# Attention scores of a sequence issued in two runs on TensorE instead of three

## The chip, the cores and the metric

The kernel runs on one core of one Trainium2 chip. A core has five engines that run side by side: TensorE (PE, matrix products), VectorE (DVE), ScalarE (ACT, functions of one variable), GpSimd (POOL) and SyncE (SP, which issues most of the DMA transfers). The metric is the device time of one execution in microseconds; the median of three executions of the kernel before is 3600.9 us (3593.78 to 3604.1).

## The reference

The input `x` is 32 sequences of 256 tokens with 256 channels. A state-space block works on it first, and then two transformer layers with local attention; the result is added to `x`.

```python
def _L0_cond_ref(x, t_emb, ...):
    xr, gate = jnp.split(x @ W_in.T, 2, axis=-1)
    ...                       # + t_emb, causal convolution of 4 taps, silu, layer norm -> xn
    def step(h, inputs):      # one step per token: 256 steps in a row
        ad, bd, xt, ct = inputs
        h = jnp.clip(h * ad[:, :, None] + bd[:, :, None] * xt[:, None, :], -10.0, 10.0)
        yt = jnp.einsum('bd,bdh->bh', ct, h)
        return (h, yt)
    ...
    return y * jax.nn.silu(gate) @ W_out.T

def _layer(x, wqkv, qs, ksc, wo, lg, lb, w1, b1, w2, b2):     # twice (DEPTH = 2)
    h = shift_token(x)
    q, k, v = jnp.split(h @ wqkv, 3, axis=-1)                 # 8 heads of 64
    q, k = l2norm(q) * qs, l2norm(k) * ksc
    q, k = rotary_xpos(q, k)
    o = local_attention(q, k, v)      # windows of 128: a query sees keys at most 128 back
    x = x + o @ wo
    h = layer_norm(shift_token(x))
    a, g = jnp.split(h @ w1 + b1, 2, axis=-1)                 # 682 wide each
    return x + (a * gelu(g)) @ w2 + b2

x = x + _L0_ffn_ref(_L0_cond_ref(x, cond, ...), ...)
```

With 256 tokens a sequence has two windows of 128. Keys of block 0 are seen by the queries of both windows, with a triangular mask in each half; keys of block 1 are seen by the queries of window 1 alone, with one triangular mask.

## The kernel before

**Tiling.** The 32 sequences form four groups of eight. The state-space block of a group is a scan of 256 steps. Each step is one VectorE instruction (`step`, L716) on a tile of 128 x 512; it needs a row of inputs that a DMA repeats over the partitions (`load_rows`, L685, tile `xrep`) and ScalarE scales (`scale_row`, L706). Four steps at a time, TensorE reads the states out into the tile `y` (`read_out`, L728). Around the scan stand its convolution (L478, L489, `th` at L504, `xc` at L509), a norm, a gate and two projections.

The two transformer layers of a group take its sequences one by one. Over the four groups that makes 64 sequence passes. They run one group behind the scan: while the sequences of group g are in attention and feed-forward, the scan of group g+1 goes on between them. The last group (`self.apart`) has no scan beside it.

**Stages.** A sequence pass takes eight stages (`ST = 8`). `stage(n, i, what)` puts a step of sequence n into stage i; a stage number of n+1, n+2 or n+3 means that the step of sequence n runs while a later one is in its attention. The stages that matter here are these:

- `turn` (stages 6 and 0): TensorE turns the queries and keys of a window; ScalarE copies them to `qT` and `kT` (L1033).
- `project` (stages 0 and 1 for window 0, 3 and 4 for window 1, of the next sequence): TensorE makes `ps_qkv` (L989), ScalarE squares it (L1002), VectorE and GpSimd rotate and normalise it (L1005 to L1022).
- `scores` (L1182): see below.
- `mask` (L1219): GpSimd clears the masked half of the second block's exponentials (L1225). In the last group VectorE does the same for the first block (L1230).
- `sums` and `values` (stage 7): TensorE sums the exponentials (`rs`, L1239) and multiplies them with the values (`ov`, L1258).
- `finish` (stage 6 of the next sequence): TensorE multiplies with `wo` (`ps_wo`, L1039).
- `normalise`, `apply`, `spread` (stages 0, 1 and 3, two sequences later): `tp_h`, `hn`, `tp_hn`, `hT`.
- `widen` for m = 0 to 5 (stages 4 to 9, two sequences later): TensorE makes `pa` (L1362), ScalarE takes the Gelu of one half (`ag`, L1373). One stage after each, `product` (L1380) on VectorE multiplies the other half into `ag`, and so ends the use of the PSUM bank of `pa`.
- `narrow` (stages 3 and 4, three sequences later): TensorE makes `po_f` (L1389), VectorE adds it to the residual (L1400).

**Scores.** A call `scores(b, kw, i0, n)` takes key block `kw` and n pairs of heads from pair i0 on. It opens two PSUM banks, one for each head of a pair, since a head has 64 channels and TensorE takes two heads side by side in the two halves of its rows. For block 0, outside the last group, a bf16 matmul first writes the mask into each bank (L1194); the products of keys and queries (L1205) then add to it in pieces of 64 keys and 192 queries. Block 1, and block 0 in the last group, have no mask in the bank and use pieces of 128 keys. Then ScalarE takes the exponentials of both banks (L1214) into tiles `pT`. A sequence has three calls: block 1 with all four pairs at stage 2, block 0 with pairs 0 and 1 at stage 3, and block 0 with pairs 2 and 3 at stage 5.

**Function tables.** [...] The exponential and the Gelu stand in different sets; where one follows the other, the built program has an instruction that loads a table (`ACT_TABLE_LOAD`).

**What sets the order.** After each stage the main loop (L1521) lets the scan advance by its share of steps, so the program's text interleaves both. The framework's scheduler then orders each engine's instructions, mostly in that order, and an engine runs its own list in order. All PSUM tiles come from one pool of eight banks (`ps_w`), used in turn: a tile's first writer waits until the last reader of the tile that had its bank is done. The six `pT` buffers hold one sequence's exponentials.

Of the kernel before, what the change touches and what calls it, by code (L numbers as in the profile page):

```python
# [10 lines left out]
FP = mybir.dt.float32  # L11
# [8 lines left out]
P = 128  # L20
S = 256
# [15 lines left out]
HEADS = 8  # L37
DH = 64
W = 128
# [13 lines left out]
def bc(ap, axis, n):  # L53

    ap = ap.unsqueeze(axis)
    shape = list(ap.shape)
    shape[axis] = n
    return ap.broadcast_to(shape)
# [15 lines left out]
def kernel(  # L74
# [29 lines left out]
    nc = tc.nc  # L104
# [72 lines left out]
    mask_t = const.tile([P, 2 * W], BF, tag="mask_t", name="mask_t")  # L177
    ident_b = const.tile([P, P], BF, tag="ident_b", name="ident_b")
# [43 lines left out]
    def program(ctx, exact):  # L222
# [9 lines left out]
        ps_w = ctx.enter_context(tc.tile_pool(name="psw", bufs=8, space=PSUM, reuse_waits="tile"))  # L232
# [921 lines left out]
        class Attention:  # L1154
# [24 lines left out]
                        self.rot.pop((b, w, a)), self.qkv[b][a][:, :, w * W : (w + 1) * W]  # L1179
                    )  # L1180

            def scores(self, b, kw, i0, n):  # L1182


                qT, kT, _ = self.qkv[b]
                nq = S - kw * W
                masked = kw == 0 and not self.apart
                nm = 2 if masked else 1
                mk = W // nm
                banks = []  # L1190
                for r in range(2):
                    sc = ps_w.tile([P, n, nq], FP, tag="w", name="sc")
                    if masked:
                        nc.tensor.matmul(  # L1194
                            sc, ident_b, bc(mask_t[:, 0:nq], 1, n), start=True, stop=False
                        )
                    banks.append(sc)
                for i in range(n):
                    for r in range(2):
                        rows = slice(r * DH, (r + 1) * DH)  # L1200
                        for m in range(nm):

                            k0 = m * mk
                            q0, q1 = (k0, k0 + W + mk) if masked else (0, nq)
                            nc.tensor.matmul(  # L1205
                                banks[r][k0 : k0 + mk, i, q0:q1],
                                kT[rows, i0 + i, kw * W + k0 : kw * W + k0 + mk],
                                qT[rows, i0 + i, kw * W + q0 : kw * W + q1],
                                start=not masked,
                                stop=not masked or i == n - 1,  # L1210
                            )
                for r in range(2):
                    p = aw.tile([P, n, nq], FP, tag="pT", name="pT", bufs=6)
                    nc.scalar.activation(p, banks[r], AF.Exp)  # L1214
                    self.ps[kw, i0, r] = p
                    for i in range(n):
                        self.p[b, kw, i0 + i, r] = p[:, i, :]
# [224 lines left out]
        def stage(n, i, what, *args):  # L1442
            stages.setdefault(ST * n + i, []).append(partial(what, *args))

        def attend(n, at, b, nxt):

            stage(n, 0, at.turn, b, 1)
            stage(n, 3, at.scores, b, 0, 0, 2)
            stage(n, 2, at.scores, b, 1, 0, HEADS // 2)
            stage(n, 5, at.scores, b, 0, 2, 2)  # L1450
            stage(n, 3, at.mask, 1, 0)
            if at.apart:
                for i, what in ((4, (0, 0)), (6, (0, 2))):
                    stage(n, i, at.mask, *what)
            stage(n, 7, at.sums, b)
            stage(n, 7, at.values, b)
            stage(n + 1, 0, at.put_inverse)
            stage(n + 1, 2, at.load_inverse)
            stage(n + 1, 4, at.divide, b)
            stage(n + 1, 6, at.finish, b)  # L1460
            if nxt is not None:
                for w in range(NW):
                    for i, a in ((0, 2), (1, 0), (1, 1)):
                        stage(n, 3 * w + i, nxt[0].project, nxt[1], w, a)
                stage(n, 6, nxt[0].turn, nxt[1], 0)
# [27 lines left out]
        for n, (g, l, b) in enumerate(seqs):  # L1493
            nxt = (ats[n + 1], seqs[n + 1][2]) if n + 1 < len(seqs) else None
            attend(n, ats[n], b, nxt)
            feed(n, g, l, b)
# [24 lines left out]
        for t in range(max(stages) + 1):  # L1521
# [3 lines left out]
            g, r = divmod(t + 1 + group - reload, group)  # L1525
# [124 lines left out]
```

## Time and profile before

| What | Value |
| --- | --- |
| Median of three executions | 3600.9 us |
| Profiled execution | 3604.19 us |
| Its span, from first to last instruction | 3602.5 us |
| TensorE busy | 3463.1 us |
| VectorE busy | 2667.7 us |
| ScalarE busy | 2148.9 us |
| GpSimd busy | 1884.7 us |
| TensorE clock granted, mean | 0.989 |

A profile row of a group of instructions gives line, engine, operation, output and inputs, shapes and count; then the busy time of the group, the mean duration of one in ns, and the time for which the engine stood idle just before them, with what ended it. In a list of waits the waiting instruction stands before the arrow, what it waited for behind it, and then the total in us, the number of times and the longest. The chain of waits starts at the last instruction and goes back, at each step to what released it or to the instruction before it on its engine. TensorE takes a float32 matmul in two passes, so the profile counts two for each.

The first 500 us belong to the scan of group 0, before any attention. From about 510 us on the 64 sequence passes follow each other; about 2630 us in, the scan of the last group is over.

### The profile page before, as it was taken

Reading aid. Unit: us, or ns where it says so; the run is one execution under the profiler, and the core shown is the slowest. Engines: PE = TensorE matmul, PEld = TensorE weight load, DVE = VectorE, ACT = ScalarE, POOL = GpSimd, SP = SyncE. Lnnn points to the kernel's source line nnn. Section 1 sums busy time; section 2 is a strip of 40 time slices with the busy share of each in tenths; the row PEclk is TensorE's granted clock in tenths of the full one; section 3 lists DMA queues with packets and bytes.
Section 4 is the critical chain, followed back from the end, with each engine's and each line's share of the span. In section 5 each row is a group of like instructions: output and inputs, shape, how many; then the busy total and the mean of one; then the engine's idle time right before and its main releaser. Section 6 shows DMA issues by size and latency. Waiting matters only on the chain.

```text
span 3602.5 us, 57609 instructions
## 1 busy us (share of the span) xinstructions
PE 3463.1 (96%) x20220; PEld 2254.4 (63%) x20220; DVE 2667.7 (74%) x5049; ACT 2148.9 (60%) x3659; POOL 1884.7 (52%) x1842
## 2 busy tenths in 40 slices
PE   7999988999999999999999999999999999999999
PEld 4545335666666666666666666666666677777777
DVE  5888889878888777887787888877877545555553
ACT  4656656666666666666666666666666544444543
POOL 4433466545556555655565556555544444443451
PEclk9999999999999999999999999999999999999999
DMA  7788755444454545444454555544454212011111
GB/s 201 210 217 219 200 154 148 133 110 138 131 140 130 149 140 146 130 114 126 117 140 128 135 149 137 142 106 130 116 141 123 61 38 61 13 30 39 31 27 37
DMA packets 468766, 435.67 MB, mean 121 GB/s; under 512 B 228723, under 2 KB 308084, under 8 KB 468340
## 3 DMA queue, kind: packets, MB, share of 16 engines
q1 hardware_dynamic: 384018, 419.88, 42.4%
q10 hardware_dynamic: 84450, 12.01, 2.0%
q8 instruction: 163, 2.67, 0.3%
q14 instruction: 135, 1.11, 0.1%
HBM read 383.54 MB, written 46.66 MB: 119 GB/s over the span
## 4 chain that ended last, share of the span: by engine, by line
PE 59%; DVE 19%; POOL 7%; DMA 7%; ACT 5%; issue 3%; SPq 0%; ACTq 0%; DVEq 0%; POOLq 0%
PE ps_qkv L989 12%; PE pa L1362 12%; DVE h L716 7%; PE po_f L1389 7%; DMA xrep<-xnd 5%; PE ps_wo L1039 4%; PE y L728 4%; PE ov L1258 3%; PE sc L1205 3%; DVE acc L489 3%; PE ps_out L808 2%; ACT xrep L706 2%; PE tr_qk L1028 2%; PE ps_in L399 2%; POOL rn L1021 2%
## 5 line engine op out<-in xcount | busy, mean ns | idle before, releaser
L716 DVE CUSTOM_DVE_ANT_0 h<-h,xrep,lim 128x512 f32<-128x512 f32 x1024 | 959.2, 937 | 219.2 <-ACT xrep L706 185.1
L706 ACT ACTIVATE xrep<-xrep,beta 128x512 f32<-128x512 f32 x960 | 674.2, 719 | 366.6 <-DMA xrep<-xnd 281.3
L989 PE MATMUL ps_qkv<-qkv,res 128*128 128x512 f32 x1536 | 718.5, 603 | 25.2 <-DVE ag L1380 9.8
L1362 PE MATMUL pa<-hT,w 128*128 128x256 f32 (+1 forms) x2816 | 679.9, 383 | 0.0
L1362 PEld LDWEIGHTS pa<-hT,w 128*128 128x128 f32 (+1 forms) x2816 | 516.2, 189 | 147.0 <-issue 53.8
L1013 POOL TENSOR_TENSOR rot<-rot,swp 128x512 f32<-128x512 f32 x256 | 340.1, 1328 | 442.7 <-DVE swp L1010 297.8
L989 PEld LDWEIGHTS ps_qkv<-qkv,res 128*128 128x128 f32 x1536 | 281.2, 191 | 314.1 <-issue 239.4
L1021 POOL TENSOR_TENSOR rn<-ss,neg_half 128x8 f32<-128x8 f32 x256 | 459.0, 1793 | 17.0 <-DVE ss L1019 6.9
L728 PE MATMUL y<-h,ly 128*32 128x512 f32 x2048 | 347.0, 611 | 18.9 <-DVE h L716 17.5
L1314 POOL TENSOR_TENSOR rstd<-ve,neg_half 128x2 f32<-128x2 f32 x64 | 47.0, 734 | 605.1 <-DVE ve L1312 587.7
L1389 PE MATMUL po_f<-ag,w 128*128 128x256 f32 x1280 | 309.7, 389 | 5.5 <-DVE fo L1400 4.3
L1022 POOL TENSOR_TENSOR rot<-rot,rn 128x512 f32<-128x512 f32 x256 | 289.3, 1130 | 19.9
L1380 DVE SCALAR_TENSOR_TENSOR ag<-pa,b_sb,ag 128x256 f32<-128x256 f32 x320 | 152.2, 476 | 195.8 <-ACT ag L1373 195.8
L1389 PEld LDWEIGHTS po_f<-ag,w 128*128 128x128 f32 x1280 | 237.3, 192 | 70.8 <-DVE xc L509 11.7
L1002 ACT ACTIVATE sq<-ps_qkv 128x512 f32<-128x512 f32 x256 | 151.9, 595 | 208.1 <-PE ps_qkv L989 145.5
L1373 ACT ACTIVATE ag<-pa,b_sb 128x256 f32<-128x256 f32 x320 | 150.1, 469 | 179.5 <-PE pa L1362 177.4
L489 DVE SCALAR_TENSOR_TENSOR acc<-xr,wc_sb,acc 128x256 f32<-128x256 f32 x384 | 197.7, 543 | 68.2 <-POOL acc L478 67.6
L1039 PE MATMUL ps_wo<-oT,wo 128*128 128x256 f32 x1024 | 231.6, 379 | 0.0
L1005 DVE TENSOR_TENSOR rot<-ps_qkv,rc_sb 128x512 f32<-128x512 f32 x256 | 174.5, 681 | 68.1 <-ACT sq L1002 67.9
L1214 ACT ACTIVATE pT<-sc 128x512 f32<-128x512 f32 x384 | 208.4, 596 | 6.8 <-PE sc L1205 4.8
L1039 PEld LDWEIGHTS ps_wo<-oT,wo 128*128 128x128 f32 x1024 | 194.6, 190 | 27.1 <-PE y L728 0.8
L1205 PEld LDWEIGHTS sc<-qT,kT 64*64 64x64 f32 (+1 forms) x2816 | 134.8, 159 | 114.6 <-issue 89.2
(159 smaller groups left out, 5689.8 us busy)
## 6 DMA issues: line engine op xcount, KB each, us to landing
xrep<-xnd SPq DMA_DIRECT2D x960, 256.0 KB
rb<-inv SPq DMA_DIRECT2D x128, 256.0 KB
xnd<-xn SPq DMA_DIRECT2D x64, 256.0 KB
qkv<-in_wqkv_dram SPq DMA_DIRECT2D x24, 512.0 KB
ahead<-xs_a SPq DMA_DIRECT2D x48, 256.0 KB
xp<-ahead SPq DMA_DIRECT2D x48, 256.0 KB
xd<-xnd SPq DMA_DIRECT2D x192, 64.0 KB
w<-in_w_dram SPq DMA_DIRECT2D x80, 128.0 KB
```

What stands on the lines that cost most here:

```text
L489: nc.vector.scalar_tensor_tensor(acc, xr[:, :, k : k + CH], wc_sb[:, ch, k : k + 1], acc, ALU.mult, ALU.add,)
L706: scaled = nc.scalar.activation(bx, ck[c].pop(("bx", t), bx), AF.Copy, scale=ck[c]["beta"][:, t : t + 1])
L716: nc.vector._custom_dve(TENSOR_ADD_SAT, out=h_new, in0=state["h"], in1=bx, s0=ck[c]["lim"][:, 0, t : t + 1], s1=ck[c]["lim"][:, 1, t : t + 1],
L728: nc.tensor.matmul(ck[c]["y", hb][32 * q : 32 * q + 32, :], ly[hb % 2][:, 32 * t : 32 * t + 32], ck[c].pop(("h", hb * TB + t)), start=(i = ...
L989: nc.tensor.matmul(ps, res[b][:, k, t0 : t0 + W], wt["qkv", a][:, k], start=(k == 0), stop=(k == KM - 1),)
L1013: nc.gpsimd.tensor_add(rot, rot, swp)
L1021: nc.gpsimd.tensor_tensor(rn, ss, neg_half, ALU.pow)
L1022: nc.gpsimd.tensor_mul(rot, rot, bc(rn, 2, DH))
L1039: nc.tensor.matmul(po[:, d], wt["wo", 0][:, c, d * P : (d + 1) * P], oT[:, c, :], start=(c == 0), stop=(c == NC_ - 1),)
L1205: nc.tensor.matmul(banks[r][k0 : k0 + mk, i, q0:q1], kT[rows, i0 + i, kw * W + k0 : kw * W + k0 + mk], qT[rows, i0 + i, kw * W + q0 : kw * ...
L1362: nc.tensor.matmul(dst[x], wt["w1", m][:, k, x], self.h[:, k], start=(k == 0), stop=(k == KM - 1),)
L1389: nc.tensor.matmul(self.po[:, d], wt["w2", 0][:, m, d * P : (d + 1) * P], self.ag[m], start=(m == 0), stop=(m == len(MCH) - 1),)
```

## The change

`scores` takes several parts at once. It opens the banks of all its parts and writes their masks (`open_banks`), then issues the products of all (`products`), and then the exponentials of all (`exponentials`). The bodies of the three are those of the old `scores`. At stage 2 the first half of block 0 goes together with block 1, block 0 first; the second half of block 0 goes from stage 5 to stage 3. In the last group the masks of block 0 move from stages 4 and 6 to stages 3 and 4. A sequence so has two runs of scores, of four banks and of two, where it had three of two banks.

```diff
-            def scores(self, b, kw, i0, n):
+            def open_banks(self, kw, n):
+                nq = S - kw * W
+                banks = []
+                for r in range(2):
+                    sc = ps_w.tile([P, n, nq], FP, tag="w", name="sc")
+                    if kw == 0 and not self.apart:
+                        nc.tensor.matmul(
+                            sc, ident_b, bc(mask_t[:, 0:nq], 1, n), start=True, stop=False
+                        )
+                    banks.append(sc)
+                return banks
+
+            def scores(self, b, *parts):
+                opened = [self.open_banks(kw, n) for kw, i0, n in parts]
+                for part, banks in zip(parts, opened):
+                    self.products(b, *part, banks)
+                for part, banks in zip(parts, opened):
+                    self.exponentials(b, *part, banks)
+
+            def products(self, b, kw, i0, n, banks):
                 qT, kT, _ = self.qkv[b]
                 nq = S - kw * W
                 masked = kw == 0 and not self.apart
                 nm = 2 if masked else 1
                 mk = W // nm
-                banks = []
-                for r in range(2):
-                    sc = ps_w.tile([P, n, nq], FP, tag="w", name="sc")
-                    if masked:
-                        nc.tensor.matmul(
-                            sc, ident_b, bc(mask_t[:, 0:nq], 1, n), start=True, stop=False
-                        )
-                    banks.append(sc)
                 for i in range(n):
...
+
+            def exponentials(self, b, kw, i0, n, banks):
+                nq = S - kw * W
                 for r in range(2):
                     p = aw.tile([P, n, nq], FP, tag="pT", name="pT", bufs=6)
                     nc.scalar.activation(p, banks[r], AF.Exp)
...
             stage(n, 0, at.turn, b, 1)
-            stage(n, 3, at.scores, b, 0, 0, 2)
-            stage(n, 2, at.scores, b, 1, 0, HEADS // 2)
-            stage(n, 5, at.scores, b, 0, 2, 2)
+            stage(n, 2, at.scores, b, (0, 0, 2), (1, 0, HEADS // 2))
+            stage(n, 3, at.scores, b, (0, 2, 2))
             stage(n, 3, at.mask, 1, 0)
             if at.apart:
-                for i, what in ((4, (0, 0)), (6, (0, 2))):
+                for i, what in ((3, (0, 0)), (4, (0, 2))):
                     stage(n, i, at.mask, *what)
```

## The prediction

> **What bounds the kernel now.** I read in turn the busy table and its 40 slices, the busy time by stretches, the waits of TensorE, ScalarE's groups, and the chain with the timelines of one pair of sequences (times of day below are from these timelines).
>
> The busy table:
>
> ```profile
> PE 3463.1 (96%) x20220; PEld 2254.4 (63%) x20220; DVE 2667.7 (74%) x5049; ACT 2148.9 (60%) x3659; POOL 1884.7 (52%) x1842
> ...
> PE   7999988999999999999999999999999999999999
> ```
>
> TensorE is the bound; only what it waits for, or streams, can move the end. By stretches, its idle time is 54 us before 500 us (attention has not begun: outside the change), 36 us from 500 to 1260, 41 us from 1260 to 2630, and 7 us afterwards. The stretch of 41 us, and what TensorE waited for in it:
>
> ```profile
> 1260.00:2630.00 1370.00, 1328.87 (x8267) 877.83 (x8260) 1097.29 (x2085) 886.34 (x1517) 793.19 (x736) 1.00 0.48 131
> ...
> PE sc L1194 <- DVE ag L1380: 18.7, 12, 2.2
> PE ps_qkv L989 <- DVE ag L1380: 9.8, 13, 0.9
> PE ov L1258 <- DVE ag L1380: 6.2, 10, 1.0
> PE ps_qkv L989 <- DVE rinv L1247: 3.1, 7, 0.5
> ```
>
> Nearly half is the mask matmul of a sequence's third score run (stage 5), which waits for a PSUM bank that `product` (L1380) frees late. It recurs every 103 us, in one of every two sequences.
>
> ScalarE's groups:
>
> ```profile
> L1214 ACT ACTIVATE pT<-sc 128x512 f32<-128x512 f32 x384 | 208.4, 596 | 6.8 <-PE sc L1205 4.8
> L1214 ACT ACT_TABLE_LOAD x124 | 159.1, 1283 | 7.1 <-PE sc L1205 4.4 <-ACT xrep L706 0.7
> L1373 ACT ACT_TABLE_LOAD x124 | 159.1, 1283 | 2.2
> ```
>
> The exponentials and the Gelu take turns: 124 loads each way for 64 sequences, about two of each per sequence, because the third run at stage 5 stands between `widen` at stages 4 and 6.
>
> The chain of waits from 1540 to 1602 us runs on TensorE to 1545.2, leaves it for VectorE, GpSimd and ScalarE, and returns at 1595.75. Some of it:
>
> ```profile
> 1578.12 0.61 ACT xrep L706
> ...
> 1578.75 1.28 ACT L1373
> ...
> 1580.54 1.83 DVE h L716
> ...
> 1587.47 3.81 DMA xrep<-xnd
> ...
> 1595.75 1.98 PE ps_qkv L989 x4
> ```
>
> VectorE's timeline there:
>
> ```profile
> 1585.79 1.66 DVE L716 CUSTOM_DVE_ANT_0 h<-h,xrep,lim 128x512 f32<-128x512 f32 x2 [1.43 <-ACT xrep L706]
> ```
>
> So for half of each pair of sequences VectorE sets the pace and TensorE just keeps up. In this pair TensorE waits 1.11 us (sc, 1570.2), 0.58 (ov, 1583.8), 0.35 and 0.86 (ps_qkv, 1589.9 and 1595.7): 2.90 us. A wait removed on TensorE alone comes back at the next of these, unless VectorE's own chain shortens.
>
> TensorE's timeline shows what a change of its array's shape costs:
>
> ```profile
> 1539.87 1.88 PE L989 MATMUL ps_qkv<-qkv,res 128*128 128x512 f32 x4
> 1541.59 1.03 PE L399 MATMUL ps_in<-xg,w_in_sb 128*128 128x256 f32 x4
> ...
> 1543.32 3.60 PE L989 MATMUL ps_qkv<-qkv,res 128*128 128x512 f32 x8
> 1546.85 1.07 PE L728 MATMUL y<-h,ly 128*32 128x512 f32 x8
> ```
>
> Four passes take 1.72 us before another full-array group, so eight take 3.44; before the 128*32 group they take 3.53. One turn of shape costs 0.09 us.
>
> **What the Trainium skill says.** "TensorEngine Tiling (Array Packing)", Key Properties: changing the tiling mode drains TensorE. The trace agrees: 0.09 us. "ScalarE: Activation LUTs", What ACT_TABLE_LOAD costs: about 1283 ns for the load and some 1380 ns more of drain. The trace agrees on the load (1283 ns in every one) and not on the drain: at 1516.73 a Gelu ends by 1517.20 and the load starts at 1517.22. The same page, Table sets: tanh is in exp's set; here a Tanh (L504) at 1555.2 follows the exponentials with no load. "PSUM — Partial Sum Buffer", Specifications: 8 banks, which is the whole pool; the trace shows the sharing as the waits above.
>
> **The change, part by part.** Products, masks, exponentials and sizes stay: 11,232 matmuls in either order of instructions. No moved step issues a DMA, so no queue is passed.
>
> *Turns of shape.* Counted in the built order: 1130 before, 1104 after. 26 x 0.09 = 2.4 us off TensorE. It is not three per sequence, because the second block's 64*128 products still differ from the masked 64*64 ones, and reads of y move into new gaps.
>
> *Table loads.* 250 become 126 in the built order: 124 x 1.283 = 159 us off ScalarE. That is cover, not path: ScalarE is 60% busy. Worth on the path: between 0 and the loads that lie on the chain.
>
> *The third run leaves stage 5.* In the pair at 1570: its wait for `ag` of m=0 (1.11 us) goes. The next user of that bank is ps_wo, after y (1.0) and pa (1.73). With the run's own 1.24 us (masks 0.43, products 0.81) now earlier in the stream, TensorE is there at 1568.7 + 1.24 + 2.73 = 1572.7. The `ag` ended at 1570.1; two xr additions (0.33 each) now stand before it: 1570.8. No wait there, but TensorE is then some 1.4 us early for the next.
>
> *ov's wait.* The `ag` that frees its bank (1583.3 to 1583.8) stands behind pd, xr, pi, ct and beta. In the new order it comes right after pd (ends 1582.6), so TensorE restarts about 1583.1, not 1583.82: 0.7 us.
>
> *The two h at 1585.79.* VectorE idled 1.43 us before them, for an xrep queued behind one that needs beta, and behind the qT and kT copies. In the new order that xrep precedes the beta one. The additions moved behind `ag` put beta at about 1584.1 (1583.4 before), and the h start at 1584.2: 1.6 us earlier. The DMA of 3.81 us, the xrep and the h behind them follow, so the `ag` before 1595.75 and TensorE's ps_qkv come at about 1594.1.
>
> That is 1.65 of 2.90 us in the pair, 57%. I take this pair for all. Over the 41.0 us of 1260 to 2630: 23.4 us. In 500 to 1260 the waits are irregular (y for h, po_f for the residual); I take 0, with bounds of -12 (a third of 36) and +12.
>
> *Four banks at once, four exponentials in a row.* The new waits: the third run's bank (or ps_qkv behind it) for the first exponential. In the pair at 1550, part one's products would end at 1551.0 and the first exponential at 1554.2 (its old place in ScalarE's row); the first waiter comes after the second block's products (1.09), half of po_f (2.59), tp_hn (0.43), a mask pair (0.43) and products (0.81), at 1556.3. 2 us to spare: 0. Behind the burst wait the th copies (L504), 0.35 us later; GpSimd, which needs their result, is busy until 1558.5 anyway. GpSimd's mask of the second block needs its exponential by 1556.0; it ends about 1555.8. The mask steps moved in the last group lie in a stretch where TensorE never waits.
>
> Sum: 23.4 + 2.4 = 25.8 us. Profiled execution: 3604.2 (span 3602.5), so 3578.4; it stood 3.3 us over the median of three, 3600.9, so **3575**.
>
> **Rivals.**
>
> *The chain holds (3598).* VectorE's chain keeps its length, the waits move to ov and ps_qkv, and only the turns are saved: 3600.9 - 2.4. For it: VectorE is nearly without a gap from 1567 to 1585. Against it: the new place of `ag` and of xrep.
>
> *All waits go (3545).* 41 + 12 + 2.4 = 55 us. For it: a table load (1.28 us) is on the chain some 15 times between 800 and 2630. Against it: ps_qkv's wait for stage 0's `ag` and rinv has nothing to do with tables.
>
> *ScalarE held up behind th (3622, slower).* In the new order, two th that wait for VectorE's acc (done at 1561.5) stand ahead of v_sb and two xrep, which before ran at 1557.7 to 1559.5. The xrep then end at 1563.5, and the h goes from 1562.45 to 1563.6: 1.15 us on the chain in each of some 20 pairs between 508 and 2630, 23 us, with nothing gained but the turns. It decides where VectorE lacks 1.15 us of other work in that place. Against it: xc and acc pieces worth 1.5 us stand there in the new order.
>
> **How the numbers follow.** The likeliest case 0.50 (3560 to 3589), all waits 0.12, the chain holds 0.24, held up 0.14. Within 0.3% (10.8 us) is what a measurement here can't tell from no change. Faster: 0.50 + 0.12 and a little of the third: 0.64; same 0.22; slower 0.14. The range leaves out half of the second case and most of the last: 3550 to 3602.
>
> **What would show it.** Right: 62 loads or so on each of the two lines; no wait of the mask matmul for `ag`; TensorE idle 17 us less or so in a stretch like 1260 to 2630, with what remains at ps_qkv and ov. Wrong: waits of sc, ps_qkv or y for pT (banks crowd), ov's wait grown to 2 us (the chain holds), or h waiting longer for xrep around stage 3 (held up).

## The result, and the profile after

The median fell from 3600.9 to 3593.1 us (17 executions of each), 7.8 us. The ratio is 0.9977, with a 95% interval of 0.9968 to 0.9987. The profiled execution took 3592.27 us, its span 3590.5 us (before: 3604.19 and 3602.5). The direction is the forecast one; the size is less than a third of the forecast 25.8 us. Executions of one kernel differ with the clock that TensorE was granted: the seventeen of the changed kernel run from 3599.84 us at a mean clock of 0.987 to 3581.01 us at 0.994. Their mean clock is 0.990. Of those of the kernel before only the profiled one has its clock on record (0.989); beside the later runs that kernel had 0.987 to 0.988 on average. So part of the 7.8 us may be clock.

The page's busy table of the changed kernel:

```profile
PE 3448.4 (96%) x20220; PEld 2253.8 (63%) x20220; DVE 2667.8 (74%) x5049; ACT 1979.5 (55%) x3535; POOL 1874.5 (52%) x1842
```

Compared with the table of before, ScalarE loses 169 us of work (2148.9 to 1979.5) and the kernel hardly notices. TensorE's busy time falls by 14.7 us, more than the span, which is 12.0 us shorter: its idle time over the whole execution (span less busy time) rose from 139.4 to 142.1 us, where the forecast had 23.4 us less.

The stretch of 1260 to 2630 us again (columns: stretch, its length, then busy time and instructions of TensorE, its weight loads, VectorE, ScalarE, GpSimd, then clock, DMA share and GB/s):

```profile
1260.00:2630.00 1370.00, 1329.11 (x8300) 880.68 (x8296) 1092.32 (x2097) 815.39 (x1471) 783.46 (x742) 1.00 0.48 131
```

What TensorE waited for there (total us, times, longest):

```profile
PE ov L1271 <- DVE ag L1393: 17.8, 13, 1.4
PE pa L1375 <- DVE zT L799: 9.1, 7, 2.0
PE ps_qkv L989 <- DVE rinv L1260: 8.2, 13, 0.9
...
PE ps_qkv L989 <- DVE ag L1393: 1.3, 2, 0.8
```

The mask's wait for `ag` (18.7 us) is gone, and that of `ps_qkv` for `ag` is down from 9.8 to 1.3 us. In their place `ov` waits 17.8 us (6.2 before), `pa` 9.1 us for `zT` (not on the list before), and `ps_qkv` 8.2 us for `rinv` (3.1 before). TensorE's idle time in the stretch is 40.9 us, against 41.1: it changed places.

ScalarE's groups of table loads:

```profile
L1227 ACT ACT_TABLE_LOAD x62 | 79.5, 1283 | 1.7 <-ACT xrep L706 0.7
L1386 ACT ACT_TABLE_LOAD x62 | 79.5, 1283 | 1.1
```

The loads are halved, 124 to 62 on each line, as counted beforehand.

The chain of waits in the same pair of sequences:

```profile
1576.62 0.23 PE tr_qk L1028 x2
1576.90 0.68 DVE zT L799
...
1581.34 1.82 DVE h L716
...
1590.34 1.99 PE ps_qkv L989 x4
```

TensorE now carries the chain up to 1576.9, where before it lost it at 1545.2; then it leaves for VectorE's `zT`, which comes too late.

**Where the 7.8 us came from.** The two traces can be laid side by side by the start of each sequence's first `rs`. The time between two such starts (sequences counted from 0; sequences 40 to 47 have hardly any scan beside them, 48 to 63 none):

| Sequences | Before, us | After | Turns of TensorE's shape | Clock granted |
| --- | --- | --- | --- | --- |
| 0 to 16 | 839.2 | +3.0 | 290 to 289 | 0.988 to 0.992 |
| 16 to 40 | 1236.6 | -7.4 | 408 to 420 | 0.996 to 1.000 |
| 40 to 48 | 359.0 | +1.2 | 113 to 111 | 1.000 |
| 48 to 63 | 577.6 | -6.0 | 164 to 134 | 1.000 |

These are single executions; ahead of the first of these starts they differ by 2.8 us more, nearly all of it in sequence 0's own stages. But the last row is firm: TensorE never waits there, and it came out the same in every kernel below that has 134 turns in it, to 0.5 us. So of the gain most comes from the last group, for which the prediction had only turns at 0.09 us each. Beside the scan, where it had 23.4 us, little is left.

The second row must be read with the clock beside it. The whole stretch, before and after, and then its first pair of sequences, before and after:

```profile
1373.08:2609.67 1236.59, 1199.96 (x7441) 792.47 (x7440) 989.60 (x1879) 799.04 (x1369) 719.54 (x666) 1.00 0.48 130
1373.32:2602.49 1229.17, 1195.36 (x7441) 793.18 (x7440) 978.78 (x1878) 733.48 (x1324) 703.66 (x664) 1.00 0.48 131
1373.08:1479.51 106.43, 101.44 (x621) 66.32 (x620) 84.72 (x159) 66.91 (x115) 64.65 (x62) 0.98 0.57 153
1373.32:1477.90 104.58, 99.79 (x622) 66.04 (x621) 82.39 (x158) 61.01 (x111) 62.01 (x60) 1.00 0.56 153
```

For the same 7441 matmuls TensorE's idle time falls by 2.8 us only (36.6 to 33.8); the other 4.6 us are busy time, although there are 12 turns more. In three of the twelve pairs (those from 1373, 1992 and 2200 us) the kernel before was granted a clock of 0.98 and the changed kernel 1.00; these three hold 6.3 of the 7.4 us, the other nine 1.1. A pair behind a slowed one makes up for some of the delay, so this is no clean division. How much of the second row is the clock, and whether the order of instructions had a part in the clock, is not shown. TensorE's waits, at which the forecast aimed, did not shrink: from the first scores to the start of sequence 40 it was idle for 75.5 us before and for 76.2 us after.

**What happened in the pair at 1570.** ScalarE of the changed kernel, and VectorE behind it:

```profile
1553.77 2.06 ACT L1227 ACTIVATE pT<-sc 128x512 f32<-128x512 f32 x4
1555.70 0.74 ACT L706 ACTIVATE xrep<-xrep,beta 128x512 f32<-128x512 f32 x1
```

```profile
1556.48 0.81 DVE L716 CUSTOM_DVE_ANT_0 h<-h,xrep,lim 128x512 f32<-128x512 f32 x1 [1.44 <-ACT xrep L706]
...
1559.29 0.48 DVE L489 SCALAR_TENSOR_TENSOR acc<-xr,wc_sb,acc 128x256 f32<-128x256 f32 x1 [0.46 <-POOL acc L478]
...
1564.14 0.48 DVE L489 SCALAR_TENSOR_TENSOR acc<-xr,wc_sb,acc 128x256 f32<-128x256 f32 x1 [0.64 <-POOL acc L478]
```

VectorE in the kernel before, at the same place:

```profile
1555.36 1.22 DVE L716 CUSTOM_DVE_ANT_0 h<-h,xrep,lim 128x512 f32<-128x512 f32 x1
...
1559.11 2.75 DVE L489 SCALAR_TENSOR_TENSOR acc<-xr,wc_sb,acc 128x256 f32<-128x256 f32 x6 [1.42 <-POOL acc L478]
...
1566.89 0.48 DVE L489 SCALAR_TENSOR_TENSOR acc<-xr,wc_sb,acc 128x256 f32<-128x256 f32 x1 [0.39 <-POOL acc L478]
...
```

The row `xrep` that the scan's next step needs was scaled between the exponentials (1554.61 before); now it stands behind all four and starts at 1555.70. The step that waits for it starts 1.1 us later (the two traces stand within 0.15 us of each other here). With one more wait of 0.30 us for `acc` in each, between or behind the lines shown, VectorE's waits here add up to 2.84 us (1.44 + 0.46 + 0.30 + 0.64), against 2.11 (1.42 + 0.39 + 0.30). Over the twelve pairs of sequences 16 to 40, VectorE's idle time in this part of the pair is 35.3 us, against 25.9: 0.78 us more per pair, on the engine of which the forecast said that it sets the pace.

### The profile page after: what moved, and what is told of

Its sections match the earlier page's. It is cut to its first block, busy times and chain, and to the rows that moved or that the text cites. A ratio compares the mean times of both kernels' runs of the same rounds, so it can differ in the third digit from the quotient of the medians.

```text
span 3590.5 us, 57544 instructions
## 1 busy us (share of the span) xinstructions
PE 3448.4 (96%) x20220; PEld 2253.8 (63%) x20220; DVE 2667.8 (74%) x5049; ACT 1979.5 (55%) x3535; POOL 1874.5 (52%) x1842
## 4 chain that ended last, share of the span: by engine, by line
PE 62%; DVE 19%; DMA 7%; POOL 5%; issue 3%; ACT 3%; SPq 1%; ACTq 0%; DVEq 0%; POOLq 0%
PE pa L1375 13%; PE ps_qkv L989 13%; DVE h L716 7%; PE po_f L1402 7%; PE ps_wo L1039 5%; DMA xrep<-xnd 5%; PE y L728 4%; PE ov L1271 3%; PE sc L1215 3%; PE ps_out L808 2%; PE ps_in L399 2%; PE tr_qk L1028 2%; PE rs L1252 2%; DVE acc L489 2%; PE ps_raw L518 1%
## 5 line engine op out<-in xcount | busy, mean ns | idle before, releaser
L1021 POOL TENSOR_TENSOR rn<-ss,neg_half 128x8 f32<-128x8 f32 x256 | 466.3, 1822 | 16.7 <-DVE ss L1019 7.0
L728 PE MATMUL y<-h,ly 128*32 128x512 f32 x2048 | 347.2, 611 | 14.9 <-DVE h L716 13.9
L1271 PE MATMUL ov<-pT,v_sb 128*64 128x256 f32 (+1 forms) x2048 | 184.3, 330 | 19.3 <-DVE ag L1393 19.3
```

The lines of the kernel that those rows point to most:

```text
L728: nc.tensor.matmul(ck[c]["y", hb][32 * q : 32 * q + 32, :], ly[hb % 2][:, 32 * t : 32 * t + 32], ck[c].pop(("h", hb * TB + t)), start=(i = ...
L1021: nc.gpsimd.tensor_tensor(rn, ss, neg_half, ALU.pow)
L1271: nc.tensor.matmul(ov[r * DH : (r + 1) * DH, i, kw * W :], self.qkv[b][2][:, kw, h * DH : (h + 1) * DH], self.p.pop((b, kw, i0 + i, r)), s ...
```

## The experiments

The theory at the start was this. Four exponentials in a row hold up a scaled row, VectorE's chain gets longer, and so most of what the change takes off TensorE beside the scan is given back; what remains is mainly the last group's turns at twice the price. Its rivals: the table loads matter; moving the run is worth nothing anyway; another wait holds VectorE as soon as this one goes. Each ratio below is to the kernel before, run beside it (its median was 3601.2 to 3604.9 us).

### The parts of the change

**Three runs, the third one early.** From the kernel before:

```diff
-            stage(n, 5, at.scores, b, 0, 2, 2)
+            stage(n, 3, at.scores, b, 0, 2, 2)
...
-                for i, what in ((4, (0, 0)), (6, (0, 2))):
+                for i, what in ((3, (0, 0)), (4, (0, 2))):
```

> The kernel before (3600.9 us) with its three runs kept apart; only the third moves from stage 5 to stage 3 (in the last group with its masks). It has 126 table loads as the changed kernel has, 1134 turns of shape (1130 before), and never four exponentials in a row. If the order without a burst lets the gain of moving the run come through (17 to 23 us as forecast, less 0.8 us for 4 turns): 3578 to 3585. If moving the run and 124 table loads fewer are worth nothing on the path: 3600 to 3603, and the whole gain of the change is its turns.

Measured: 3602.5 us, ratio 0.9993 (0.9985 to 1.0001). Neither number: the last group took 6.0 us less here too (the two runs of block 0 now touch, so it has 134 turns as well), and beside the scan some 3 us were lost in its trace. There is no burst ahead of the scaled row here, but VectorE's waits for GpSimd's `acc` rose from 25 to 32 us over the twelve pairs. The place alone gains nothing that the time shows.

**Joined, the rest left at stage 5.** From the changed kernel:

```diff
-            stage(n, 3, at.scores, b, (0, 2, 2))
+            stage(n, 5, at.scores, b, (0, 2, 2))
...
-                for i, what in ((3, (0, 0)), (4, (0, 2))):
+                for i, what in ((4, (0, 0)), (6, (0, 2))):
```

> The first half of block 0 joined to the second block at stage 2, as in the change, but the second half of block 0 stays at stage 5: 250 table loads as before and 1068 turns of shape (before 1130, after 1104). With a turn at 0.197 us (0.093 at the change and 0.104 at the first step in the new shape, read from the last group of both traces) 62 turns are 12.2 us: 3588.7 where turns alone count, less if the wait for the third run's bank takes some back. With a turn at 0.09 us, the forecast's price, 5.6 us: 3595. Burst theory: the four exponentials in a row are here too, so VectorE's two h wait about 1.4 us for a scaled row in every second sequence and 10 to 20 us of this come back: 3595 to 3609.

Measured: ratio 1.0002 (0.9994 to 1.0010). It has 62 turns fewer than before, and its last group took 5.5 us less; the time shows nothing of it. Joining alone gains nothing either. The burst theory forecast this, and its wait of 1.4 us behind the exponentials is there in each pair (17.3 us over twelve). But the trace does not bear it out as the cause: in sequences 16 to 40, where these pairs are, the kernel took some 3 us less than the kernel before (with a clock of 0.999 there, against 0.996). It lost 5.9 us between the first scores and sequence 16, and 8.7 us ahead of the first scores, where the two kernels have the same work.

**The change in the last group alone, and in the other three alone.**

```diff
+            if at.apart:
                 stage(n, 2, at.scores, b, (0, 0, 2), (1, 0, HEADS // 2))
                 stage(n, 3, at.scores, b, (0, 2, 2))
+            else:
+                stage(n, 3, at.scores, b, (0, 0, 2))
+                stage(n, 2, at.scores, b, (1, 0, HEADS // 2))
+                stage(n, 5, at.scores, b, (0, 2, 2))
```

The second kernel has the two branches exchanged, and the last group's masks at their old stages.

> The change in the last group alone (16 of 64 sequences, no scan beside them); the others as before. 1098 turns of shape (before 1130), 218 table loads. In four new orders so far the last group took 5.54 to 5.98 us less between its first and its sixteenth sequence than in the kernel before, with TensorE never idle and 30 turns fewer there. Theory that the gain of the change is the turns of its last group, at 0.199 us each: 32 turns, 6.4 us less than before, ratio 0.9982. Theory that the groups beside the scan give most of it: at most 2 us less, ratio 0.9995.

> The change in the first three groups alone (48 sequences, with the scan beside the first 40); the last group as before. 1136 turns of shape, 158 table loads. Theory that the gain is the last group's turns: what the change gave in all (7.8 us) less 6.4 is 1.4 us, ratio 0.9996, no change that can be told. Theory that the third run's wait and place gave the gain: 6 us less or more, ratio 0.9983 or below.

Measured: the last group alone 0.9979 (0.9968 to 0.9991), the first three alone 0.9994 (0.9983 to 1.0004). The two add up to the changed kernel's 0.9977 within their intervals. Nearly all of the gain is the last group; what the change does beside the scan can't be told from nothing by the time. The traces show no waits of TensorE removed: from the first scores to sequence 40 it was idle for 74.5 us with the old order there and for 76.9 us with the new. Sequences 16 to 40 took 1235.5 and 1229.8 us, but again with three pairs at a clock of 0.98 in the old order and none in the new.

**One run in the last group.** From the changed kernel:

```diff
+            if at.apart:
+                stage(n, 2, at.scores, b, (0, 0, 2), (1, 0, HEADS // 2), (0, 2, 2))
```

> The changed kernel, but in the last group all six banks of a sequence are one run at stage 2, with six exponentials behind it: 1072 turns of shape (the changed kernel 1104), 126 table loads. With a turn at 0.199 us, 32 fewer are 6.4 us less than the changed kernel, ratio to the kernel before 0.9960; with a turn at 0.09 us 2.9 us, ratio 0.9969. If six banks at once of eight leave the next tiles without one, TensorE waits up to 1 us in each of 16 sequences: ratio 0.998 to 1.000.

Measured: ratio 0.9955 (0.9941 to 0.9968). From the first to the sixteenth sequence of the group TensorE had 104 turns and took 566.15 us, where the changed kernel has 134 and 571.65, and the kernel before 164 and 577.63: 0.183 and 0.199 us per turn. Six banks at once cost nothing that shows there. TensorE's timeline shows where a turn's price lies. Before:

```profile
3021.40 1.16 PE L1205 MATMUL sc<-qT,kT 64*128 64x128 f32 x16
3022.49 2.42 PE L1389 MATMUL po_f<-ag,w 128*128 128x256 f32 x10
...
3025.72 1.14 PE L1205 MATMUL sc<-qT,kT 64*128 64x256 f32 x8
3026.78 1.98 PE L989 MATMUL ps_qkv<-qkv,res 128*128 128x512 f32 x4
3028.60 2.32 PE L1389 MATMUL po_f<-ag,w 128*128 128x256 f32 x10
```

After, and then with one run:

```profile
3014.97 2.02 PE L1215 MATMUL sc<-qT,kT 64*128 64x256 f32 x24
3016.93 2.43 PE L1402 MATMUL po_f<-ag,w 128*128 128x256 f32 x10
```

```profile
3018.88 2.89 PE L1215 MATMUL sc<-qT,kT 64*128 64x256 f32 x32
3021.70 2.43 PE L1402 MATMUL po_f<-ag,w 128*128 128x256 f32 x10
```

By their starts, the two runs of before last 1.09 and 1.06 us, and joined 1.96: 0.19 less for the same 24 products. With the third run, of the second's form (1.06), they last 2.82, again 0.20 less. Outside the run, `po_f` x10 takes 2.42 after a run of scores and 2.32 after a full-array group. So a turn is paid twice: about 0.09 us at the last step in the old shape, which the prediction saw, and about 0.10 us at the first step in the new one, which it did not.

### The table loads

From the changed kernel, an exponential of one column more per sequence, called at stage 5:

```diff
+            def touch(self):
+                t = aw.tile([P, 1], FP, tag="touch", name="touch")
+                tc.keep_in_program_order(nc.scalar.activation(t, one, AF.Exp))
```

> The changed kernel (3593.1 us) with one more exponential, of one column and with no reader, at stage 5 of each sequence: it brings two table loads per sequence back (250 instead of 126), 159 us of ScalarE and nothing on TensorE. If the loads are cover, as forecast: 3593 to 3596. If about one load per pair of sequences lies on the path (20 pairs at 1.28 us): about 3618. If each counts: 3750.

Its groups of loads on ScalarE:

```profile
L1390 ACT ACT_TABLE_LOAD x124 | 159.1, 1283 | 2.2
L1227 ACT ACT_TABLE_LOAD x62 | 79.5, 1283 | 1.7 <-ACT xrep L706 0.7
L1234 ACT ACT_TABLE_LOAD x62 | 79.5, 1283 | 1.1
```

Measured: ratio 0.9964 (0.9952 to 0.9977). All 159 us are back, and the kernel is no slower than the changed one. The loads were cover, or nearly so. ScalarE's order moved a little as well, and in sequences 16 to 40 TensorE's idle time fell from 33.8 to 26.0 us for a reason that was not followed; a cost of a few us may hide behind that. One load per pair on the path, some 26 us in all, is ruled out.

### The two waits of VectorE

**Exponentials of the second block late.** From the changed kernel:

```diff
-                for part, banks in zip(parts, opened):
-                    self.exponentials(b, *part, banks)
+                self.late = list(zip(parts, opened))
+                self.exps(b)
...
+            stage(n, 3, at.exps, b)
             stage(n, 3, at.scores, b, (0, 2, 2))
```

The new `exps` takes the exponentials of one part per call.

> The changed kernel (3593.1 us), but the two exponentials of the second block are issued at stage 3, ahead of those of the second run, and no longer right behind the two of the first half of block 0: two in a row where there were four. The turns of shape (1104) and table loads (126) stay; on ScalarE one row of the scan is scaled between the two pairs. Burst theory: behind four exponentials (2.06 us) the scaled row came late and VectorE's two h waited about 1.44 us for it in every second sequence, so its chain ran about 1 us late; this wait goes, and the time falls by 0.5 to 1.0 us in each of about 20 pairs, 10 to 20 us: 3573 to 3583. Theory that only TensorE's streaming counts, and waits only change places: 3590 to 3596. A later exponential could also free its bank late and cost TensorE up to 0.5 us per sequence: up to 3610.

Measured: ratio 0.9973 (0.9962 to 0.9985), the changed kernel's. VectorE's timeline in the same pair:

```profile
1559.30 1.24 DVE L716 CUSTOM_DVE_ANT_0 h<-h,xrep,lim 128x512 f32<-128x512 f32 x1 [0.47 <-ACT xrep L706]
...
1563.07 0.48 DVE L489 SCALAR_TENSOR_TENSOR acc<-xr,wc_sb,acc 128x256 f32<-128x256 f32 x1 [1.08 <-POOL acc L478]
...
1567.91 0.48 DVE L489 SCALAR_TENSOR_TENSOR acc<-xr,wc_sb,acc 128x256 f32<-128x256 f32 x1 [0.64 <-POOL acc L478]
```

The wait for the scaled row fell from 1.44 to 0.47 us, as meant, and the wait for GpSimd's `acc` took over, 1.08 us where it was 0.46. With two more of 0.30 us among the lines left out, the sum is 2.79 us against 2.84. The burst theory had its cause right and its consequence wrong: VectorE has two waits here, and when this one went the other grew. GpSimd's `acc` is late because GpSimd clears the second block's masked half (1.75 us in the changed kernel) just before it.

**Clearing later.** From the changed kernel, and again from the one with late exponentials:

```diff
-            stage(n, 3, at.mask, 1, 0)
+            stage(n, 3 if at.apart else 5, at.mask, 1, 0)
```

> The changed kernel, but outside the last group GpSimd clears the masked half of the second block at stage 5, not 3. The orders of TensorE, VectorE and ScalarE are those of the changed kernel; on GpSimd the two clearings (1.75 us) now stand behind the first tap of the convolution (acc), not ahead of it. In the changed kernel VectorE waits in each second sequence 1.44 us for a scaled row behind four exponentials and 1.3 us for GpSimd's acc. Here the second goes in part, the first stays: if VectorE sets the pace there, 0.3 to 1.0 us in each of 20 pairs, 6 to 20 us under the changed kernel: ratio to the kernel before 0.992 to 0.996. If VectorE's waits are not what sets the pace: 0.9977 as the changed kernel. If the clearings hold up GpSimd's rotations of the next queries and keys by 1.75 us and TensorE's turning of them waits: up to 1.004.

> Late exponentials and late clearing together: the second block's exponentials at stage 3 (so that a scaled row goes between the pairs) and GpSimd's clearing at stage 5. With the late exponentials alone VectorE's wait for the scaled row fell from 17.3 to 2.3 us over twelve pairs and its wait for GpSimd's acc rose from 16 to 26 us, and the time stood still (ratio 0.9973). If these two waits in turn set VectorE's pace, and VectorE that of TensorE beside the scan, both go here: 1.5 to 2.5 us in each of 20 pairs, ratio 0.985 to 0.990. If another chain holds the pace (the scan's rows by DMA, the norm's statistics by GpSimd), 0.995 to 0.998. If GpSimd's rotations come late: up to 1.004.

Measured: the clearing alone 0.9986 (0.9979 to 0.9993), both together 0.9948 (0.9935 to 0.9962). With both, VectorE in that pair:

```profile
1560.00 1.23 DVE L716 CUSTOM_DVE_ANT_0 h<-h,xrep,lim 128x512 f32<-128x512 f32 x1 [0.46 <-ACT xrep L706]
...
1563.49 2.07 DVE L489 SCALAR_TENSOR_TENSOR acc<-xr,wc_sb,acc 128x256 f32<-128x256 f32 x5 [0.46 <-POOL acc L478]
...
1567.55 0.48 DVE L489 SCALAR_TENSOR_TENSOR acc<-xr,wc_sb,acc 128x256 f32<-128x256 f32 x1 [0.64 <-POOL acc L478]
...
```

With one of 0.30 us behind them that is 1.86 us in all, and 22.7 over twelve pairs (the changed kernel 35.3, either move alone 34.0 and 35.3). Either move alone leaves VectorE's waits as they were and makes nothing faster; together they take 0.29% more off than the change, about 10 us, of which the traces show 9.3 in sequences 16 to 40. So it is shown that two things hold VectorE up in this place, the burst and the clearing, that either alone keeps its waits where they were, and that removing both saves time. What the clearing does alone is less settled: in its trace TensorE's idle time in sequences 16 to 40 fell from 33.8 to 29.2 us, but the clock there was 0.994 on average (the changed kernel had 1.000), and the length stayed. The gain of both is less than the 1.5 to 2.5 us per pair that was expected. One reason is a new wait of TensorE:

```profile
PE rs L1256 <- POOL pT L1242: 22.4, 26, 1.4
```

Its sums now wait for the clearing itself, which at stage 5 stands behind GpSimd's rotations.

**Clearing between two rotations.** To remove this third wait, the clearing goes to stage 4, ahead of the second of the two rotations there; then the same with the last group's one run; and the same move in the kernel before. The first two keep the late exponentials.

```diff
-            stage(n, 3, at.mask, 1, 0)
+            if at.apart:
+                stage(n, 3, at.mask, 1, 0)
...
                         stage(n, 3 * w + i, nxt[0].project, nxt[1], w, a)
+                        if not at.apart and (w, a) == (1, 0):
+                            stage(n, 4, at.mask, 1, 0)
```

> As with late exponentials and late clearing together (ratio 0.9948), but GpSimd clears between the rotations of the next keys and queries of window 1, earlier than there, where TensorE's sums (rs) waited 20.4 us over twelve pairs for the clearing. TensorE, VectorE and ScalarE keep their orders. If this was a wait that TensorE alone paid: 1.0 to 1.7 us in each of 20 pairs, ratio 0.985 to 0.989. If it only took the place of another wait (ov for ag, rinv): 0.994 to 0.996. If the second rotation, now 1.75 us later, holds up TensorE's turning: 0.996 to 0.999.

> The kernel of the expectation before this, and in the last group one run of all six banks at stage 2, which gave 7.9 us over the changed kernel by itself (0.9977 to 0.9955). If the two add: 0.0020 to 0.0022 below that kernel's ratio, and faster than both the kernel before and the changed one by 15 us or more.

> The kernel before with GpSimd's clearing alone moved, outside the last group, to between the rotations of window 1; three runs as before. VectorE waits 25 us over twelve pairs for GpSimd's acc in the kernel before. If VectorE's waits set the pace by themselves, also with the third run at stage 5: 0.5 to 1.5 us in each of 20 pairs, ratio 0.992 to 0.997. If the third run's wait for its bank holds TensorE however early VectorE is, or VectorE only waits at the next place: 0.999 to 1.001, and what late clearing gave was part of what the change could have given.

Measured, in this order: 0.9931 (0.9917 to 0.9945), 0.9931 (0.9918 to 0.9945) and 0.9972 (0.9964 to 0.9980). The first of them waits in 1260 to 2630 us for:

```profile
PE ov L1275 <- ACT xn L579: 12.0, 13, 1.1
```

The wait for the clearing is gone, and `ov` has one again, for the bank of a state-space tile that ScalarE reads. The gain, 0.0017 below the kernel ahead of it, is less than the two intervals together. Nor is it where the wait was: sequences 16 to 40 took 1223.6 us here and 1219.9 us there, with TensorE idle for 29.6 and 24.4 us, while the mean clock of the executions was 0.991 here and 0.987 there. So taking this wait away gained nothing that is shown.

The third kernel corrects the story. Clearing later gives the kernel before, with its three runs, some 10 us without any of the change (0.28%; medians 3601.2 and 3591.8 us). Against that, the change with both moves gives 0.9931 / 0.9972 = 0.9959, about 15 us. The two traces differ by 13.9 us: 6.0 in the last group, 4.1 ahead of sequence 0's first `rs`, and 4.1 in sequences 16 to 40, where both had the full clock: 0.34 us per pair. (The kernel with late exponentials and the clearing at stage 5 took 7.7 us less there than the kernel before with its clearing moved: 0.64 us per pair.) TensorE's idle time from the first scores to sequence 40 is the same, 66.6 us before the change and 66.7 with it. So the forecast 1.65 us per pair was not merely eaten by these two waits; even without them most of it isn't there.

The version with one run in the last group has the lowest median, 3574.0 us, 27.3 us under the kernel before beside it, and beats both kernels. That it beats its neighbour (3577.3 us) the time doesn't show. The trace does for that stretch: 566.15 us, as in the one-run kernel above.

### Added work on TensorE

From the changed kernel, in the even or in the odd sequences of the first three groups (where `self.again` is set), for the second run:

```diff
+                times = 4 if self.again and len(parts) == 1 else 1
...
+                        for j in range(times):
                             nc.tensor.matmul(
-                                sc, ident_b, ..., start=True, stop=False
+                                sc, ident_b, ..., start=True, stop=j < times - 1
                             )
```

> The changed kernel with work added on TensorE: in the even sequences of the first three groups each mask product of the second run is done four times, of which the first three are overwritten: 144 products of 0.215 us, 1.29 us in each of 24 sequences, 31 us in all. It stands at stage 3 of the half in which TensorE waits (2.8 us per pair). If VectorE sets the pace there, it is hidden but for what the three pairs without a wait show: 0 to 8 us over the changed kernel, ratio to the kernel before 0.9977 to 1.0000. If TensorE sets the pace: 31 us, ratio 1.0064.

> The same 144 added products of 0.215 us, but in the odd sequences, in whose half TensorE hardly waits. If each pair has one half that TensorE paces and one that VectorE paces, the added time delays what VectorE gets in this half as well: 20 to 31 us over the changed kernel, ratio to the kernel before 1.003 to 1.0064. If VectorE sets the pace in both halves: 0 to 8 us, ratio 0.9977 to 1.0000.

Measured: 1.0027 (1.0018 to 1.0036) and 1.0028 (1.0017 to 1.0040). Both are 18 us over the changed kernel (0.0050 and 0.0051), of 31 us added: 58%, in whichever half. In sequences 16 to 40 the traces even show 12.8 us (even) and 14.9 us (odd, of which up to 1.7 may be one stretch of 3.4 us at half the clock) of the 15.5 added, while TensorE's idle time there fell from 33.8 to 31.2 and 31.7 us only. So the half in which TensorE waits 2.8 us per pair doesn't hide 1.29 us; its waits are no slack that lies there. The picture of a half paced by VectorE and one paced by TensorE is refuted. What the runs fit is one loop in which TensorE and VectorE wait for each other, but the loop itself was not traced, nor how the rest is absorbed.

## Why the prediction was right or wrong

- **Table loads.** Right: 62 per line, and cover. Putting all 159 us back cost nothing that the time shows.
- **The third run leaves stage 5.** Right as far as it went: the wait of `sc` for `ag` is gone, `ps_wo` does not wait, and TensorE came early to the next place. What it found there was not worked out. It is `pa` on `zT` (9.1 us in 1260 to 2630), which VectorE started at 1576.90 where it had been 1575.77.
- **ov's wait.** Wrong. `ag` does come right after `pd`, 0.8 us sooner than in the old order; but `pd` itself started 0.8 us late (1583.09, before 1582.30). `ag` started at 1583.28, at 1583.29 before, where the forecast had 1582.6; the difference is about the 0.73 us by which VectorE's waits had grown. `ov`'s total wait rose to 17.8 us.
- **The two h at 1585.79.** Right in kind: the first of them started at 1584.73, 1.1 us earlier and not 1.6.
- **Four banks at once, four exponentials in a row.** This is the step that failed first. It was costed at nothing, with the banks, `th` and GpSimd's clearing looked at. The scaled row that stood between the exponentials before was not, though the list of ScalarE's instructions showed it; nor was GpSimd's `acc`, which with `th` and the clearing ahead of it comes too late as soon as VectorE is on time. Together 0.78 us per pair on VectorE. Removing only one of the two made nothing faster, removing both gave 10 us.
- **"I take this pair for all."** The second failed step, and by the runs the larger. The pair itself gained about 1.1 us of the 1.65 (`y` at 1596.55, 1597.66 before). Over the twelve pairs of sequences 16 to 40 TensorE's idle time fell by 2.8 us, 0.24 us per pair; the whole gain there, clock included, is 7.4 / 12 = 0.62 us. The sixteen sequences ahead lost 3.0 us, and all three groups together gave 0.06%, not told from nothing. So the term of 23.4 us, the waits of TensorE that were to go, came to nothing: from the first scores to sequence 40 they are 75.5 us before and 76.2 after. Behind it stands the claim that TensorE "just keeps up" in half of each pair, so that VectorE's earlier instructions come through whole: the added work refutes it, and with the two waits of VectorE out of the way the change is worth 0.34 us per pair.
- **500 to 1260 us, taken as 0 with bounds of 12.** Within the bounds: from the first scores to sequence 16 the changed kernel took 0.4 us more. TensorE's waits there did grow, by several small ones (`pa` for `zT`, `ov` for `ag`, scores for an exponential that still holds a bank). This isn't chance: in the three traces with the changed kernel's order beside the scan (the changed kernel, the first three groups alone, one run in the last group) it was idle for 42.2 to 42.5 us, in the two with the old order for 38.9 and 38.3. Why `zT` comes late was not followed.
- **Turns of shape.** The mechanism was right, the size was off: 0.19 us by the last group, not 0.09, because the first step in the new shape pays again. The count was also spread wrongly. The last group saves 32 turns, the others gain 6; 32 at 0.199 are 6.4 us, most of the whole gain, where the sum had 2.4. Beside the scan a turn is not paid one for one: the kernel joined at stage 5 has 30 fewer there, and its time shows no gain. That the direction of the forecast came right is owed mostly to this term, a tenth of its sum; in that the forecast was lucky.
- **The rivals.** "The chain holds" (3598) came closest: the waits moved to `ov`, as it said, though `pa` and `rinv` took as much as it did, and `ov`'s longest wait was 1.4 us, short of the 2 us named as its sign. "ScalarE held up behind th" had the right engine and the wrong place. The `th` do stand ahead of `v_sb` and two rows, and VectorE had pieces of `xc` and `acc` to do meanwhile, as its counter-argument said; the row it waited for was the one ahead, behind the exponentials. "All waits go" was far off.

## What to carry to other kernels

When a change puts several instructions of one kind in a row on an engine, look up what stood between them before and who waits for it; that instruction may be the price. An engine that waits need not have slack where it waits: add a known amount of work there and see how much comes out before counting on it, and before extending one pair to all. Where two causes are each enough to hold an engine up, removing one shows nothing; remove both before dropping the theory. And before a difference of a few us between two traces is put down to an edit, compare the granted clock in the same stretch of both, and see whether the engine's idle time or its busy time has changed.

## What was unexpected of the hardware

In the last group a turn of TensorE's shape costs about 0.19 us in all, half at the last step in the old shape and half at the first step in the new: 30 turns fewer gave 5.98 us, 30 more fewer gave 5.50 us, with TensorE idle for 0.14 us at most. "TensorEngine Tiling (Array Packing)", Key Properties, of the Trainium skill speaks of the drain when the mode changes; the traces show that it is felt on both sides of the change. And 124 table loads, 159 us of ScalarE's time at 55% busy, were put back with no loss that the time shows (0.9964 with them, 0.9977 without).
